# Four-layer convolution chain on one core: one output block a step, and a statistics pass that scales on GpSimd

## The chip, the cores and the metric

The kernel runs on one core of a Trainium2 chip. A core has TensorE (PE, matrix products into PSUM), VectorE (DVE), ScalarE (ACT), GpSimd (POOL), and SyncE (SP), whose queue issues nearly all DMAs here. The metric is device time in microseconds: 6498.27 us, the median of three runs (6492.53 to 6499.6). The profile is one further execution.

## The reference, cut to what matters

An image batch x of shape (4, 16, 512, 512) in float32 passes through four layers.

```python
x = layer0(x)    # depthwise 3x3 + windowed attention (8x8 windows) + MLP
# layer 1: fake-quantised 3x3 convolution, batch norm over the whole batch, clip
xq = fake_quant(x)                 # step = max|x| / 127, rounded
y  = conv3x3(xq, fake_quant(weight))
mean, var = mean(y, (0, 2, 3)), var(y, (0, 2, 3))
inv = gamma * rsqrt(var + 1e-5)
x  = clip(y * inv + (beta - mean * inv), 0, 6)
# layer 2: residual pair of convolutions
x  = conv3x3(relu(conv3x3(x, w1) + b1), w2) + b2 + x
# layer 3: convolution, then a two-layer pointwise network, residual
y  = conv3x3(x, conv_w)
x  = x + w2 @ relu(w1 @ y + b1) + b2       # 16 -> 128 -> 16 channels
```

Layer 1 needs the mean and variance of its convolution over the whole batch before any of its outputs can be normalised, so its convolution is computed twice: once for the statistics and once for the values.

## The kernel before, in words

The kernel has three stages. The first (`window_attention`, not touched) computes layer 0 and leaves its result in DRAM as `x1`, in 65 blocks of 128 partitions x 4 x 512 f32 (1 MB): `x1[mm]`. It also leaves per-partition maxima, from which `quant_step` gets the quantisation scale. A second path for large inputs isn't taken in the profiled run.

The **statistics pass** (the loop over `mm` in `conv_layers`, lines 992 to 1010) takes the 64 row blocks one after the other. `load(mm)` brings a block into one of four buffers (two tags, `x` and `o`, of two buffers each); `scaled(mm)` multiplies by the inverse step and adds a rounding constant, in place, on VectorE (L984, 128x2048); `rounded(mm)` takes the constant off again and writes bf16 into the ring `q` of three buffers, on ScalarE (L987). Then 24 turns (`_conv_turn`, L908) of four 32x32 products make the convolution of the block pair (mm, mm+1) in four PSUM banks; odd and even blocks use the two halves of PSUM. Four `bn_stats` (L1009) on VectorE read the banks. A load four blocks ahead is issued at the start of each turn of the loop. After the loop two edge blocks are loaded and scaled, and `bn_aggr` and some 1-column operations make `scale` and `shift`.

The **tail** (the loop over `t`, from `LATE, EARLY = ...` to the end of `conv_layers`) runs layers 1 to 3 as one software pipeline over the 64 blocks. A step has four groups, each of which is written by `group(conv, unit, between, at)`:

- group 1 ("x" below, after the tile that its convolution reads): layer 3's convolution, block t-4; its banks are copied to `y` by `done3`, two on VectorE, two on ScalarE;
- group 2 ("h"): layer 2's second convolution, block t-3; `done2` adds bias and `z` into `x` (four operations on VectorE, L1084). After it, `turned` issues 16 DMAs that transpose strips of `x` into `xi`, a ring of three;
- group 3 ("z"): layer 2's first convolution, block t-1; `done1` writes `h`, two on each engine;
- group 4 ("q"): layer 1's convolution again, block t, in bf16; `done0` writes `z` with Relu, scale and shift, all four strips on ScalarE (L1054). The upper clip follows in group 1 of the next step (`clipped`, L1060, VectorE).

All four convolutions use the same four banks, `conv_banks`. Each group also holds one *unit* of the pointwise network: the hidden layer of one strip of four, eight `hidden` calls of four products each (L1117) into `hid_banks`, used in turn, whose Relu goes to ScalarE five times (L1123) and to VectorE three times (L1125) out of eight. A group has 32 places on TensorE; `at` says which eight hold a hidden call, the other 24 being convolution turns. The place i also picks the row group i % 4 of the systolic array:

```python
    LATE, EARLY = range(4, 28, 3), (0, 1, 2, 3, 9, 12, 15, 18)
```

Groups 1 and 3 are LATE, groups 2 and 4 EARLY. When two units are ready, `outputs` (at the end of groups 2 and 4) makes their two output strips in `hid_banks[0:2]` (L1133, 16 products), and VectorE adds bias and the residual `xi` into a tile `o` (L1139); after the fourth strip SP stores the tile.

The order of the instructions on PE, DVE, ACT and SP is the order of the program text (a manual schedule); GpSimd, too, runs in order. Each engine stops at the first instruction whose semaphore isn't there yet.

Of the kernel before, what the change touches and what calls it, by code (L numbers as in the profile page):

```python
# [11 lines left out]
F32 = mybir.dt.float32  # L12
BF16 = mybir.dt.bfloat16
AF = mybir.ActivationFunctionType
ALU = mybir.AluOpType
# [8 lines left out]
B, C, H, W = 4, 16, 512, 512  # L24
P = 128
HR = H // 2
WP = W + 2
# [85 lines left out]
@with_exitstack  # L113
def conv_chain(ctx: ExitStack, tc: tile.TileContext, x, xw, mats, vecs, cqs, cws, hots, out):
    nc = tc.nc
    const = ctx.enter_context(tc.tile_pool(name="const", bufs=1))
    dram = ctx.enter_context(tc.tile_pool(name="dram", bufs=1, space=DRAM))

    x1 = dram.tile([M + 1, P, S, W], F32, name="x1")
    zero = const.tile([C, W], F32, name="zero")
    nc.vector.memset(zero, 0.0)
    for b in range(B):
        at = 32 * b
        nc.sync.dma_start(x1[0, at : at + C, 0], zero)
        nc.sync.dma_start(x1[M, at + C : at + 2 * C, S - 1], zero)
# [788 lines left out]
def conv_layers(ctx: ExitStack, tc, x1, out, cw, cq, sw, m, v, peak):  # L916
# [23 lines left out]
    banks = [ps.tile([P, W], F32, name=f"tb{i}") for i in range(8)]  # L940
    conv_banks, hid_banks = banks[0:4], banks[4:8]

    def ring(name, n, dt=F32):
        tiles = []
        for i in range(n):
            t = act.tile([P, 4, WP], dt, name=f"{name}{i}")
            nc.gpsimd.memset(t[:, :, 0 : WP : WP - 1], 0.0)
            tiles.append(t)
        return lambda mm: tiles[mm % n]

    qs = ring("q", 3, BF16)
    zs, hs, xs, xi, ys = ring("z", 3), ring("h", 2), ring("x", 2), ring("xi", 3), ring("y", 3)

    edge_b1 = act.tile([P, 2], F32, name="edge_b1")
# [14 lines left out]
    def inner(t):  # L969
        return t[:, :, 1 : W + 1]  # L970
# [4 lines left out]

    loaded = {}

    def load(mm, tag="x"):
        loaded[mm] = ld.tile([P, S, W], F32, tag=tag, name=f"tx{mm}")
        _load_pairs(nc, loaded[mm], x1, mm)  # L980

    def scaled(mm, at=slice(0, S)):
        t = loaded[mm][:, at]
        nc.vector.tensor_scalar(t, t, ix, ROUND, ALU.mult, ALU.add)  # L984

    def rounded(mm, at=slice(0, S)):
        nc.scalar.activation(  # L987
# [1 line left out]
        )  # L989


    tags = ("x", "o")
    for mm in range(4):
        load(mm, tags[mm % 2])
    sx, ix = quant_step(nc, act, act, peak, "x")
    for mm in range(2):
        scaled(mm)
        rounded(mm)
    for mm in range(M):
        if mm + 4 <= M:  # L1000
            load(mm + 4, tags[mm % 2])
        if mm + 2 <= M:
            scaled(mm + 2)
            rounded(mm + 2)
        p = banks[4 * (mm % 2) : 4 * (mm % 2) + 4]
        for turn in _turns():
            _conv_turn(nc, p, cq, (qs(mm), qs(mm + 1)), *turn)
        for b in range(B):
            nc.vector.bn_stats(stats[:, mm * B + b, :], p[b])  # L1009
    for mm in (-2, -1):  # L1010
        load(mm)
        scaled(mm)
        rounded(mm)
# [15 lines left out]

    own = act.tile([P, 2], F32, name="own")  # L1030
    nc.vector.bn_aggr(own, stats.rearrange("p r s -> p (r s)"))
    mean = over_strips(own[:, 0:1], "mean")
    off = act.tile([P, 1], F32, name="off")
    nc.vector.tensor_tensor(off, own[:, 0:1], mean, ALU.subtract)
# [15 lines left out]


    def done0(mm):
        for b, p in enumerate(conv_banks):
            nc.scalar.activation(  # L1054
                inner(zs(mm))[:, b], p, AF.Relu, bias=shift, scale=scale
            )

    def clipped(mm, b):
        z = inner(zs(mm))
        nc.vector.tensor_scalar(z[:, b], z[:, b], ACT_MAX, None, ALU.min)  # L1060
        if outside(mm) is not None:
            nc.vector.memset(z[_quad(outside(mm)), b], 0.0)

# [46 lines left out]
    waiting, outs = [], {}  # L1110

    def hidden(mm, s, par, b):

        k = next(count)
        p = hid_banks[k % 4]
        for c in range(4):
            nc.tensor.matmul(  # L1117
                p[_quad(c)], w1[_quad(b), 1 - par, 32 * c : 32 * c + 32],
                inner(ys(mm + par))[_quad(b), s, :], start=True, stop=True,
            )  # L1120
        hd = ld.tile([P, W], F32, tag="hid", name=f"hid{mm}_{s}_{par}_{b}", bufs=16)
        if k % 8 in (0, 2, 3, 5, 6):
            nc.scalar.activation(hd, p, AF.Relu, bias=v("l3_b1"))  # L1123
        else:
            nc.vector.tensor_scalar(hd, p, v("l3_b1"), 0.0, ALU.add, ALU.max)  # L1125
        return b, par, hd

    def outputs():

        for p in hid_banks[0:2]:  # L1130
            mm, s, hids = waiting.pop(0)
            for b, par, hd in hids:
                nc.tensor.matmul(  # L1133
                    p[_quad(b), :], w2[:, par], hd, start=par == 0, stop=par == 1
                )
            if s == 0:
                outs["o"] = ld.tile([P, S, W], F32, tag="o", name=f"o{mm}")
            o = outs["o"]
            nc.vector.scalar_tensor_tensor(  # L1139
                o[:, s, :], p, v("l3_b2"), inner(xi(mm))[:, s, :], ALU.add, ALU.add  # L1140
            )
            if s == S - 1:
                nc.sync.dma_start(out[mm], o)

    def group(conv, unit, between, at):


        turns, hids = iter(_turns() if conv else []), []
        for i in range(32):
            if i in at:  # L1150
                if unit:
                    hids.append(hidden(*unit, len(hids) // 4, i % 4))
                if between:
                    between.pop(0)()
            elif conv:
                _conv_turn(nc, conv_banks, conv[0], conv[1], *next(turns))
        for f in between:
            f()
        if conv:
# [14 lines left out]
    for t in range(-2, M + 7):  # L1174
        if t + 3 <= M + 2:
# [159 lines left out]
```

## Time and profile before

| what | before |
|---|---|
| median of the runs shown | 6498.27 us |
| time of the profiled execution | 6499.56 us |
| its span | 6497.8 us |
| PE / PE weight load | 6264.0 us (96%) / 3402.1 us (52%) |
| VectorE / ScalarE / GpSimd | 3186.5 us (49%) / 4179.7 us (64%) / 6.0 us |
| statistics pass, first scaling to last statistic | 3566.4 to 3805.4 us |
| first convolution of the tail to the end | 3817.9 to 6497.8 us |
| mean granted TensorE clock | 0.981 |

Busy times are sums over the whole span, and the three stages have different limits, so the shares of the whole say little of one stage. A row of the timeline gives the start in us from the span's start, the length, engine, line, operation, tiles (out<-in), shape and count, and in brackets how long the engine was idle before it and what ended that. Matmuls overlap in the array [...], and an f32 product of 512 columns leaves two records. A row of the waits gives the total in us, the number of times, and the longest.

### The profile page before, as it was taken

Reading aid. Unit: us, or ns where it says so; the run is one execution under the profiler, and the core shown is the slowest. Engines: PE = TensorE matmul, PEld = TensorE weight load, DVE = VectorE, ACT = ScalarE, POOL = GpSimd, SP = SyncE. Lnnn points to the kernel's source line nnn. Section 1 sums busy time; section 2 is a strip of 40 time slices with the busy share of each in tenths; the row PEclk is TensorE's granted clock in tenths of the full one; section 3 lists DMA queues with packets and bytes.
Section 4 is the critical chain, followed back from the end, with each engine's and each line's share of the span. In section 5 each row is a group of like instructions: output and inputs, shape, how many; then the busy total and the mean of one; then the engine's idle time right before and its main releaser. Section 6 shows DMA issues by size and latency. Waiting matters only on the chain. (4 is left out here: it accounts for less than half of the span.)

```text
span 6497.8 us, 317055 instructions
## 1 busy us (share of the span) xinstructions
PE 6264.0 (96%) x146976; PEld 3402.1 (52%) x146976; DVE 3186.5 (49%) x4640; ACT 4179.7 (64%) x5738; POOL 6.0 (0%) x26
## 2 busy tenths in 40 slices
PE   8999999999999999999997669999999999999999
PEld 5555555555555555555553335455555554555553
DVE  3444444444444444444443974544445554545554
ACT  5777777777777777777775544555555555555554
POOL 0000000000000000000000000000000000000000
PEclk9999999999999999999997879999999999999999
DMA  3333333333333333333322842222222222222221
GB/s 82 62 71 62 71 63 70 63 70 63 70 63 70 63 70 62 71 61 72 60 56 61 298 161 75 81 82 86 83 82 81 82 83 82 84 83 81 81 65 48
DMA packets 544390, 515.30 MB, mean 79 GB/s; under 512 B 349008, under 2 KB 480208, under 8 KB 514384
## 3 DMA queue, kind: packets, MB, share of 16 engines
q1 hardware_dynamic: 542768, 494.52, 29.2%
q8 instruction: 1154, 18.91, 1.2%
q14 instruction: 180, 1.47, 0.1%
q10 hardware_dynamic: 288, 0.39, 0.0%
HBM read 225.87 MB, written 134.48 MB: 55 GB/s over the span
## 5 line engine op out<-in xcount | busy, mean ns | idle before, releaser
L1123 ACT ACTIVATE hid<-tb,vec 128x512 f32<-128x512 f32 x1280 | 847.5, 687 | 1127.8 <-PE tb L1117 1126.5
L1117 PE MATMUL tb<-y,mat 32*32 32x512 f32 x16384 | 1567.9, 599 | 2.0 <-DVE o L1139 1.3
L367 ACT ACTIVATE e<-pair 128x1024 f32<-128x1024 f32 x1024 | 992.3, 1021 | 225.0 <-PE pair L359 224.3
L1125 DVE TENSOR_SCALAR hid<-tb,vec 128x512 f32<-128x512 f32 x768 | 575.3, 749 | 890.0 <-PE tb L1117 872.8
L295 PE MATMUL pair<-x,taps 32*32 32x512 f32 x18432 | 965.8, 605 | 1.9 <-ACT y L306 1.3
L416 PE MATMUL bank<-y,fc_e 32*32 32x512 f32 x8192 | 878.4, 607 | 3.7 <-ACT hid L421 3.2
L421 ACT ACTIVATE hid<-bank,f1b 128x512 f32<-128x512 f32 x1024 | 679.6, 686 | 298.8 <-PE bank L416 285.3
L351 DVE COPY yt<-bank 128x512 f32<-128x512 f32 x512 | 353.8, 691 | 906.1 <-PE bank L346 905.8
L359 PE MATMUL pair<-g,y 32*128 32x128 f32 x16384 | 651.2, 285 | 40.4 <-ACT e L367 39.3
L1117 PEld LDWEIGHTS tb<-y,mat 32*32 32x32 f32 x16384 | 496.4, 103 | 329.4 <-issue 185.0
L908 PE MATMUL tb<-z,cw 32*32 32x512 f32 x12864 | 640.4, 603 | 4.2 <-ACT z L1054 3.4
L359 PEld LDWEIGHTS pair<-g,y 32*128 32x128 f32 x16384 | 540.2, 186 | 186.8 <-ACT e L367 109.2
L908 PE MATMUL tb<-x,cw 32*32 32x512 f32 x12480 | 620.0, 597 | 1.5 <-ACT z L1054 1.5
L295 PEld LDWEIGHTS pair<-x,taps 32*32 32x32 f32 x18432 | 459.3, 103 | 286.3 <-issue 182.9
L908 PE MATMUL tb<-h,cw 32*32 32x512 f32 x12672 | 590.7, 601 | 1.8 <-ACT z L1054 1.5
L378 PE MATMUL bank<-e,yt 128*32 128x128 f32 x16384 | 555.3, 276 | 0.9 <-ACT r L393 0.9
L908 PE MATMUL tb<-q,cq 32*32 32x512 bf16 x12672 | 418.5, 424 | 138.4 <-ACT q L987 103.2
L383 PE MATMUL bank<-e,hot 128*32 128x512 f32 x4096 | 535.0, 593 | 0.0
L378 PEld LDWEIGHTS bank<-e,yt 128*32 128x32 f32 x16384 | 417.6, 109 | 108.1 <-DVE yt L351 52.8
L1133 PE MATMUL tb<-hid,mat 128*32 128x512 f32 x4096 | 471.1, 601 | 0.0
L429 DVE TENSOR_TENSOR xo<-bank,y 128x512 f32<-128x512 f32 x256 | 177.1, 692 | 547.2 <-PE bank L427 545.5
L346 PEld LDWEIGHTS bank<-mat,y 128*128 128x128 f32 x2048 | 215.3, 141 | 431.7 <-issue 378.1
(150 smaller groups left out, 6661.2 us busy)
## 6 DMA issues: line engine op xcount, KB each, us to landing
tx<-x SPq DMA_DIRECT2D x128, 1024.0 KB
x<-in_xw_dram SPq DMA_DIRECT2D x32, 2600.0 KB
y<-y SPq DMA_DIRECT2D x2048, 32.0 KB
xi<-x SPq DMA_DIRECT2D x1024, 64.0 KB
out_dram<-o SPq DMA_DIRECT2D x64, 1024.0 KB
x<-xo SPq DMA_DIRECT2D x2000, 32.0 KB
tx<-x SPq DMA_DIRECT2D x4, 768.0 KB
x<-xo SPq DMA_DIRECT2D x48, 24.0 KB
```

Source lines behind the costliest of these rows:

```text
L295: nc.tensor.matmul(bank(u)[quad(vv)], taps[quad(u), tap, :], xts[n // 2][quad(u), vv, dy : dy + WS, at : at + BW], start=tap == 0, stop=ta ...
L359: nc.tensor.matmul(bank(u)[:, P * jj : P * jj + P], y2[quad(u), vv, jl + jj].rearrange("p w t -> p (w t)"), g[quad(u), vv, jl + jj].rearra ...
L367: nc.scalar.activation(e[:, 2 * i : 2 * i + 2].rearrange("p u j t -> p u (j t)"), pairs[i], AF.Exp,)
L378: nc.tensor.matmul(b[quad(u), P * jj : P * jj + P], yt[:, jj, quad(u)], e[:, u, jj, :], start=True, stop=True,)
L383: nc.tensor.matmul(d[quad(u)], own, e[:, u].rearrange("p j t -> p (j t)"), start=True, stop=True,)
L416: nc.tensor.matmul(b[quad(k)], fc1[quad(vv), quad(k)], y[quad(vv), u, :], start=True, stop=True,)
L421: nc.scalar.activation(hd, b, AF.Gelu, bias=f1b)
L908: nc.tensor.matmul(p[i][_quad(j)], weights[_quad(i), side, dx, :], src[side][_quad(i), j, dx : dx + W], start=side == 0 and dx == 0, stop= ...
L1117: nc.tensor.matmul(p[_quad(c)], w1[_quad(b), 1 - par, 32 * c : 32 * c + 32], inner(ys(mm + par))[_quad(b), s, :], start=True, stop=True,)
L1123: nc.scalar.activation(hd, p, AF.Relu, bias=v("l3_b1"))
L1125: nc.vector.tensor_scalar(hd, p, v("l3_b1"), 0.0, ALU.add, ALU.max)
L1133: nc.tensor.matmul(p[_quad(b), :], w2[:, par], hd, start=par == 0, stop=par == 1)
```

## The change

In the tail, `outputs` is called once a step, when four units are ready, which is at the end of group 2. It uses all four hidden banks, adds into `xi` in place, and stores from there; the tile `o` is gone, and the ring of hidden tiles has 32 buffers instead of 16. Group 1 becomes EARLY. `done0` writes two strips on ScalarE and two on VectorE, without the lower clip, which `clipped` takes over in the same instruction.

In the statistics pass the scaling from block 2 on is done by GpSimd; the loads go to eight buffers, which are the tiles of the rings `y`, `xi` and `x` (idle in this pass), eight blocks ahead, and are issued at the end of each turn of the loop. The statistics live in the first tile of ring `h`. The zero borders of those rings are therefore written after the pass. A small tile of zeros is released early.

```diff
-    stats = act.tile([P, M * B, 6], F32, name="stats")
+    stats = rings["h"][0].rearrange("p s x -> p (s x)")[:, 0 : M * B * 6].rearrange(
+        "p (r s) -> p r s", s=6
+    )
...
-    def load(mm, tag="x"):
-        loaded[mm] = ld.tile([P, S, W], F32, tag=tag, name=f"tx{mm}")
+    def load(mm, t=None):
+        if t is None:
+            t = ld.tile([P, S, W], F32, tag="x", name=f"tx{mm}")
+        loaded[mm] = t
         _load_pairs(nc, loaded[mm], x1, mm)
 
-    def scaled(mm, at=slice(0, S)):
+    def scaled(mm, at=slice(0, S), engine=nc.vector):
         t = loaded[mm][:, at]
-        nc.vector.tensor_scalar(t, t, ix, ROUND, ALU.mult, ALU.add)
+        engine.tensor_scalar(t, t, ix, ROUND, ALU.mult, ALU.add)
...
-    tags = ("x", "o")
-    for mm in range(4):
-        load(mm, tags[mm % 2])
+    flat = [
+        t.rearrange("p s x -> p (s x)")[:, 0 : S * W].rearrange("p (s x) -> p s x", x=W)
+        for t in rings["y"] + rings["xi"] + rings["x"]
+    ]
+    AHEAD = len(flat)
+    for mm in range(AHEAD):
+        load(mm, flat[mm])
     sx, ix = quant_step(nc, act, act, peak, "x")
     for mm in range(2):
         scaled(mm)
         rounded(mm)
     for mm in range(M):
-        if mm + 4 <= M:
-            load(mm + 4, tags[mm % 2])
         if mm + 2 <= M:
-            scaled(mm + 2)
+            scaled(mm + 2, engine=nc.gpsimd)
             rounded(mm + 2)
         p = banks[4 * (mm % 2) : 4 * (mm % 2) + 4]
         for turn in _turns():
             _conv_turn(nc, p, cq, (qs(mm), qs(mm + 1)), *turn)
         for b in range(B):
             nc.vector.bn_stats(stats[:, mm * B + b, :], p[b])
+        if mm + AHEAD <= M:
+            load(mm + AHEAD, flat[mm % AHEAD])
+    for name in ("x", "xi", "y"):
+        border(name)
...
     def done0(mm):
+        z = inner(zs(mm))
         for b, p in enumerate(conv_banks):
-            nc.scalar.activation(
-                inner(zs(mm))[:, b], p, AF.Relu, bias=shift, scale=scale
-            )
+            if b % 2:
+                nc.vector.tensor_scalar(z[:, b], p, scale, shift, ALU.mult, ALU.add)
+            else:
+                nc.scalar.activation(z[:, b], p, AF.Identity, bias=shift, scale=scale)
 
     def clipped(mm, b):
         z = inner(zs(mm))
-        nc.vector.tensor_scalar(z[:, b], z[:, b], ACT_MAX, None, ALU.min)
+        nc.vector.tensor_scalar(z[:, b], z[:, b], ACT_MAX, 0.0, ALU.min, ALU.max)
...
-        hd = ld.tile([P, W], F32, tag="hid", name=f"hid{mm}_{s}_{par}_{b}", bufs=16)
+        hd = ld.tile([P, W], F32, tag="hid", name=f"hid{mm}_{s}_{par}_{b}", bufs=32)
...
     def outputs():
 
-        for p in hid_banks[0:2]:
+        for p in hid_banks:
             mm, s, hids = waiting.pop(0)
             for b, par, hd in hids:
                 nc.tensor.matmul(
                     p[_quad(b), :], w2[:, par], hd, start=par == 0, stop=par == 1
                 )
-            if s == 0:
-                outs["o"] = ld.tile([P, S, W], F32, tag="o", name=f"o{mm}")
-            o = outs["o"]
+            o = inner(xi(mm))
             nc.vector.scalar_tensor_tensor(
-                o[:, s, :], p, v("l3_b2"), inner(xi(mm))[:, s, :], ALU.add, ALU.add
+                o[:, s, :], p, v("l3_b2"), o[:, s, :], ALU.add, ALU.add
             )
-            if s == S - 1:
-                nc.sync.dma_start(out[mm], o)
+        nc.sync.dma_start(out[mm], o)
...
-        if len(waiting) == 2:
+        if len(waiting) == S:
             outputs()
...
         group(
             conv(2, xs, mm - 1, done3, mm) if 0 <= mm <= M else None,
             (t - 6, 2) if 0 <= t - 6 < M else None,
-            clip if -2 <= t - 1 <= M + 1 else [], LATE,
+            clip if -2 <= t - 1 <= M + 1 else [], EARLY,
         )
```

More of the change, by code (lines that the diff above doesn't have):

```diff
@@ L121, in conv_chain @@
     x1 = dram.tile([M + 1, P, S, W], F32, name="x1")
[L122 to L127, printed above, removed]
+    with tc.tile_pool(name="zeros", bufs=1) as one:
+        zero = one.tile([C, W], F32, name="zero")
+        nc.vector.memset(zero, 0.0)
+        for b in range(B):
+            at = 32 * b
+            nc.sync.dma_start(x1[0, at : at + C, 0], zero)
+            nc.sync.dma_start(x1[M, at + C : at + 2 * C, S - 1], zero)
     mat = const.tile([P, N_MAT], F32, name="mat")
@@ L941, in conv_layers, with border @@
     conv_banks, hid_banks = banks[0:4], banks[4:8]
+    rings = {}
     def ring(name, n, dt=F32):
-        tiles = []
-        for i in range(n):
-            t = act.tile([P, 4, WP], dt, name=f"{name}{i}")
+        tiles = rings[name] = [
+            act.tile([P, 4, WP], dt, name=f"{name}{i}") for i in range(n)
+        ]
+        return lambda mm: tiles[mm % n]
+    def border(name):
+        for t in rings[name]:
             nc.gpsimd.memset(t[:, :, 0 : WP : WP - 1], 0.0)
-            tiles.append(t)
-        return lambda mm: tiles[mm % n]
     qs = ring("q", 3, BF16)
     zs, hs, xs, xi, ys = ring("z", 3), ring("h", 2), ring("x", 2), ring("xi", 3), ring("y", 3)
+    for name in "qz":
+        border(name)
     edge_b1 = act.tile([P, 2], F32, name="edge_b1")
@@ L989, in rounded @@
         )
-    tags = ("x", "o")
-    for mm in range(4):
-        load(mm, tags[mm % 2])
+    flat = [
+        t.rearrange("p s x -> p (s x)")[:, 0 : S * W].rearrange("p (s x) -> p s x", x=W)
+        for t in rings["y"] + rings["xi"] + rings["x"]
+    ]
+    AHEAD = len(flat)
+    for mm in range(AHEAD):
+        load(mm, flat[mm])
     sx, ix = quant_step(nc, act, act, peak, "x")
@@ L1009, in conv_layers @@
             nc.vector.bn_stats(stats[:, mm * B + b, :], p[b])
+        if mm + AHEAD <= M:
+            load(mm + AHEAD, flat[mm % AHEAD])
+    for name in ("x", "xi", "y"):
+        border(name)
     for mm in (-2, -1):
@@ L1031, in conv_layers @@
     nc.vector.bn_aggr(own, stats.rearrange("p r s -> p (r s)"))
+    border("h")
     mean = over_strips(own[:, 0:1], "mean")
@@ L1109, in conv_layers @@
     count = iter(range(1 << 30))
-    waiting, outs = [], {}
+    waiting = []
     def hidden(mm, s, par, b):
```

## The prediction

> **What bounds the kernel now.** I read the page first (engine shares, the 40 slices, the chain), then the waits, DMA and timeline of the statistics pass, then TensorE's timeline over one step of the tail. From the page:
>
> ```profile
> span 6497.8 us, 317055 instructions
> PE   8999999999999999999997669999999999999999
> L279 POOL MEMSET y<- 128x4096 f32 x1 | 3.5, 3518 | 0.0
> ```
>
> TensorE is full everywhere except in slices 22 to 24, the statistics pass. So two readings are needed: what paces that pass, and what TensorE does in the tail, where it never rests. The waits, the DMA throughput (40 slices of 6.35 us) and the timeline of the pass (3561 to 3815 us):
>
> ```profile
> ACT q L987 <- DVE tx L984: 110.2, 47, 37.0
> PE tb L908 <- ACT q L987: 103.2, 50, 35.3
> GB/s 285 415 417 319 274 286 303 272 277 320 281 277 292 319 303 280 279 307 292 264 299 310 308 277 281 328 302 266 272 314 297 276 288 314 306 279 120 91 125 255
> 3594.79 1.27 DVE L984 TENSOR_SCALAR tx<-tx,inv_x 128x2048 f32<-128x2048 f32 x1
> 3595.98 2.48 DVE L1009 BATCH_NORM_STATS2 stats<-tb 128x6 f32<-128x512 f32 x4
> 3596.18 2.00 ACT L987 ACTIVATE q<-tx,unround 128x2048 bf16<-128x2048 f32 x1 [2.12 <-DVE tx L984]
> 3802.87 2.49 DVE L1009 BATCH_NORM_STATS2 stats<-tb 128x6 f32<-128x512 f32 x4 [1.32 <-PE tb L908]
> ```
>
> ScalarE waits for VectorE, TensorE for ScalarE: VectorE leads. It does one scaling (1.27 us) and four statistics (2.48 us, overlapping a little) a step, and the statistics of step 1 start at 3577.31, of step 63 at 3802.87: 3.64 us a step. The loads are not the limit: they run at about 290 GB/s, but at 415 to 417 in the two slices in which four were outstanding. From the first scaling (3566.38) to the last statistic (3805.36) the pass takes 239 us. The tail, one step on TensorE (starts of the groups; the first records of a group's own convolution or output block):
>
> ```profile
> 5083.41 0.69 PE L908 MATMUL tb<-x,cw 32*32 32x512 f32 x13
> 5093.09 0.66 PE L908 MATMUL tb<-h,cw 32*32 32x512 f32 x4
> 5102.01 0.64 PE L1133 MATMUL tb<-hid,mat 128*32 128x512 f32 x4
> 5105.59 0.76 PE L908 MATMUL tb<-z,cw 32*32 32x512 f32 x15
> 5115.26 0.41 PE L908 MATMUL tb<-q,cq 32*32 32x512 bf16 x4
> 5119.94 0.64 PE L1133 MATMUL tb<-hid,mat 128*32 128x512 f32 x4
> 5123.51 0.69 PE L908 MATMUL tb<-x,cw 32*32 32x512 f32 x13
> ```
>
> Step 40.10 us: group x 9.68, h 8.92, output block 3.58, z 9.67, q 4.68, output block 3.57. x, h and z have the same matrix work (24 convolution turns, 8 hidden products), yet the LATE groups x and z take 9.68 and the EARLY group h 8.92. ScalarE idles ahead of the hidden evictions in x (3.1 us before the first), so no product waits for one there, the 0.76 us is how the hidden products' row groups fall among the convolution's.
>
> **What the Trainium skill says.** "GPSIMD Engine Reference", § 3.1: a body of at most two arithmetic operations moves 1.03 cycles an element, while a two-input add of 2048 f32 measured 4497 ns; § 7 of the same page speaks of about 1.9 cycles for packed reads. The trace's only long GpSimd instruction, the memset of 4096 elements in 3518 ns, is 0.86 ns an element, which at the page's 1.2 GHz is 1.03 cycles; it reads nothing, so it agrees without deciding. "SBUF — State Buffer", § Who interferes with whom: GpSimd and VectorE share a port pair as an exclusive lock, but a VectorE operation with at most one SBUF input outside the two-port modes doesn't take it. The statistics read PSUM, so I expect no lock in the pass; no run here shows it yet.
>
> **The change part by part.**
>
> *Statistics pass.* 63 of the 65 scalings move to GpSimd (the first two and the two after the pass stay on VectorE). VectorE is left with 2.48 us a step, ScalarE 2.0, TensorE 96 products in about 1.7. The loads' floor is 1.049 MB at 417 GB/s = 2.51 us. GpSimd's scaling isn't in the trace. Lower bound, from memset: 128 elements took 205 ns and 4096 took 3518, so 2048 come to about 1.8 us. Upper bound: the page's two-input 4.5 us; between them 1.9 cycles, 3.2 us. I take 1.8, since one input is read and two operations done; then the loads set the step. New length: first landing 3566.4, 64 further tiles at 2.51 = 161, then the last tile's scaling 1.8, rounding 2.0, half a convolution 1.0, statistics 2.5: ends at 3734.7 instead of 3805.4, **71 us less**. At 3.2 us GpSimd sets the step: it starts at 3571.2 (third landing), 63 x 3.2 = 202, plus 5.5: 3779, 27 less. At 4.5: 3860, 55 more. The pass breaks even at 3.63 us.
> Eight buffers instead of four: a load waits for the rounding of the tile eight before it, about 4 us after that one landed, so some six loads stay queued; this only makes the 2.51 reachable. SP issues nothing else here. Left ring-border memsets (0.1 us each) follow the pass on GpSimd, hidden by the two scalings on VectorE and the 7.1 us aggregate. The two edge loads have their own buffers and are hidden behind the last tile's chain.
>
> *Group x from LATE to EARLY.* Saves 9.68 - 8.92 = 0.76 us in each of 64 steps if it packs as h does.
>
> *Output block moved.* The block after q goes; the one after h doubles to 7.14 us. Sum unchanged. But the block after q covered the evictions of z (L1054, four on ScalarE, 2.79 us from 5079.77). Now x's four leading hidden products cover 0.89 us. The eviction is split: ScalarE 2 x 0.69, VectorE 2 x 0.75 as in its other PSUM additions. VectorE is busy with the last hidden tile until 5080.09 (5079.34 + 0.75), so the fourth bank comes free at 5081.6, some 1.1 us after x's first turn would want it. Group h lives with nearly that today: its predecessor's copies (L1103 2 x 0.69 from 5092.88, L1105) free its fourth bank about 0.9 us late, inside the 8.92. So I charge 0.2 us a step for the slightly longer evictions and for the clips (0.42 each), which now queue in VectorE ahead of the second hidden tile as the scalings (0.48 each) do in h. Net 0.56 x 64 = **36 us less**. If the whole 1.1 us shows, the step gains nothing (-0.3 x 64 = 22 us worse); if nothing shows, 49 less.
> The first six steps have no outputs; there z's eviction is open today (3.0 us of TensorE idle at 3823.76), and halving it gives about 1 us in four of them: **4 less**.
>
> *Costed at nothing.* Relu's lower bound moves into the clip: same instruction. VectorE gains 2 x 0.75 us a step and is half busy. Hidden tiles live longer in 32 buffers; the next write comes after the block has read the first of them. Banks 0 to 3: z is LATE, its first hidden product comes four turns after the block. Output summed in place: the turned copies of the next tile into the same buffer, directly behind in SP's queue, must wait for the store. Store issued 8.1 us after h ends (block 7.14, eviction 0.75), 4.7 us to land (as the last one: issued 6493.1, end 6497.8), then sixteen copies in 14.3 us, then the next load: at 28 of a step of 39.5 us. The load has a step and a half before its scaling, the copies have three steps. If stores took 15 us longer, the load would begin to matter.
>
> **Sum**, against the profiled execution (6499.56 us, 1.3 above the median shown): 6499.6 - 71 - 36 - 4 = 6388.6; I say **6388**.
>
> **Rivals.**
> 1. *GpSimd paces the pass at 2.6 to 4.2 us.* For it: the 1.9 cycles; against: memset's rate. At 3.2: 6499.6 - 27 - 40 = 6433.
> 2. *Slower than before: GpSimd's scaling costs the two-input price or more.* With the tail's 40 us gained, the whole breaks even at (239 + 40 - 10.3) / 63 = 4.26 us; at 4.5 us it is 6499.6 + 55 - 40 = 6515, at 6 us about 6609. For it: software on the cores; against: one input only.
> 3. *The lost cover eats the tail's gain*: z's fourth bank and the second hidden tile late together. The step stays near 40.1: 6499.6 - 71 = 6429; for it: the queue on VectorE above; against: h does this today.
> 4. *Eight loads do not hold 417 GB/s* and stay at 290: the pass remains at 3.6 and only the tail gains: 6460. Against: the first four loads.
>
> **How the numbers follow.** Forecast 0.52; rival 1 0.22, rival 3 0.08, rival 4 0.03; rival 2 0.15 (a few hundredths of it within 0.2%, about 13 us, which is what a measurement of this kernel can tell from no change). Faster 0.83, same 0.03, slower 0.14. The range runs from 6366 (pass as forecast, tail 22 us better: no stall at x and a shorter h-like group) to 6460, which takes in rivals 1, 3 and 4; only rival 2 and small tails are left out.
>
> **What would show it.** Right: GpSimd rows of 128x2048 near 1.8 us, the pass's DMA row near 415 GB/s throughout, statistics 2.5 us apart, the pass some 71 us shorter; in the tail a step near 39.5 us with x about 9.1 and one block of 7.14. Wrong: ScalarE waiting for GpSimd in the pass, statistics further apart than 2.6 us; x as long as before, with TensorE or its weight loads waiting for VectorE's z; SP's load late, with VectorE's scaling waiting for it.

## The result and the profile after

| | before | after |
|---|---|---|
| median of five runs | 6497.87 us (6492.31 to 6499.6) | 6469.1 us (6465.19 to 6479.63) |
| profiled execution / span | 6499.56 / 6497.8 us | 6479.63 / 6477.8 us |
| first scaling to last statistic | 239.0 us | 258.8 us (forecast 168) |
| last statistic to the end | 2692.4 us | 2645.2 us (forecast 2652) |
| statistics, start to start, per step | 3.64 us | 3.93 us (forecast 2.51) |
| granted TensorE clock, 3600 to 3740 us | 0.82 | 0.71 |

The ratio after to before is 0.9963 [0.9952, 0.9974]: 29 us faster by the medians, not the 111 us of the forecast. The tail gave about what was expected. The statistics pass, which should have become 71 us shorter, became 20 us longer. (In the two profiled executions the attention stage, which the change doesn't touch, runs 8.7 us apart after its first 200 us; over all the profiled executions of this study the first scaling starts between 3566.4 and 3578.4 us. So the stages are compared here, not the spans. The three parts do add up: +7.5 until the first scaling, +19.8, -47.2 make the -19.9 us between the two executions.)

From the page of the kernel after: the span, the engines' busy time and instructions, TensorE's row and its granted clock in 40 slices, and the instruction queue's row (packets, MB, share of 16 engines).

```profile
span 6477.8 us, 317011 instructions
PE 6215.1 (96%) x146976; PEld 3422.4 (53%) x146976; DVE 3208.4 (50%) x4713; ACT 4062.8 (63%) x5602; POOL 130.9 (2%) x89
PE   8999999999999999999998569999999999999999
PEclk9999999999999999999998679999999999999999
q8 instruction: 1154, 18.91, 1.2%
```

TensorE's dip in slices 22 to 24 is still there: 8, 5 and 6 tenths where before had 7, 6 and 6. The last row is one that the prediction didn't read; it is the one that explains the pass.

The group of GpSimd's scaling in the kernel after (busy time in all, mean ns of one, idle time before them and what ended it):

```profile
L996 POOL TENSOR_SCALAR xi<-xi,inv_x 128x2048 f32<-128x2048 f32 x24 | 47.4, 1974 | 43.8 <-DMA xi<-x 43.8
```

One scaling takes 1.97 us, near the 1.8 us of the forecast, and GpSimd then waits for its data. It paces nothing. What does is in the waits of the pass, 3600 to 3790 us (total us, times, longest), kernel after:

```profile
PEld L909 <- issue: 103.2, 59, 4.5
ACT q L999 <- PE tb L909: 94.2, 38, 4.2
PE tb L909 <- issue: 79.8, 35, 4.2
DVE h L1024 <- PE tb L909: 76.5, 36, 3.9
POOL xi L996 <- DMA xi<-x: 41.2, 20, 3.8
```

and of the kernel before, same window:

```profile
PEld L908 <- issue: 109.7, 90, 2.5
ACT q L987 <- DVE tx L984: 60.8, 38, 2.1
PE tb L908 <- ACT q L987: 58.4, 42, 2.1
PE tb L908 <- issue: 16.7, 17, 1.5
```

The weight loads (PEld) wait for "issue" about as long in both; the products don't. Before, the order of waiting was TensorE on ScalarE on VectorE. After, it is reversed: ScalarE and VectorE wait for TensorE, GpSimd waits for the loads, whose buffers ScalarE frees; and TensorE, at the head of it all, waits 79.8 us in 190 for "issue", that is for nothing with a semaphore. TensorE's timeline of the kernel after shows the form of these waits (start, length, engine, line, operation, tiles, count, and in brackets the idle time before):

```profile
3683.39 3.64 PE L909 MATMUL tb<-q,cq 32*32 32x512 bf16 x128 [2.23 <-issue]
3688.51 3.64 PE L909 MATMUL tb<-q,cq 32*32 32x512 bf16 x128 [1.47 <-issue]
3699.29 3.58 PE L909 MATMUL tb<-q,cq 32*32 32x512 bf16 x128 [2.56 <-issue]
3703.58 2.06 PE L909 MATMUL tb<-q,cq 32*32 32x512 bf16 x128 [0.71 <-issue]
```

A step has 96 products, but TensorE stops after 128. The transfers of the instruction queue show why. Each is 16384 bytes, and its 18.91 MB over the whole execution, divided by the 146976 products and as many weight loads of the page, are 64.3 bytes for each of them: one transfer holds about 128 products and their 128 weight loads. The starts of six of them, set against the starts of the bursts:

```
fetch starts    burst starts    between
3681.02         3683.39         2.37
3686.27         3688.51         2.24
3691.46         3693.90         2.44
3696.88         3699.29         2.41
3701.32         3703.58         2.26
3707.24         3709.52         2.28
```

So TensorE's program is itself DMA traffic, one fetch for every 128 products, and 0.75 of a fetch a step. In the pass after, a fetch comes every 5.43 us: 0.75 x 5.43 = 4.07 us. That is the step in this stretch: 3296 products in 3600 to 3740 us (shown further below) make 140 x 96 / 3296 = 4.08 us; the 3.93 is the mean over the whole pass. This agreement is only counting, since every kernel fetches what it executes. That TensorE waits for the fetches is seen in the waits themselves: in 3600 to 3790 us there are 35 fetches and 35 waits of TensorE for "issue"; every wait ends 2.2 to 2.6 us after a fetch has started, exactly 128 products after the wait before it. The share of the loads is in the DMA view of the same window:

```profile
DMA packets 7296, 53.38 MB, mean 281 GB/s; under 512 B 815, under 2 KB 815, under 8 KB 815
q1 hardware_dynamic: 7257, 52.78, 74.0%
q8 instruction: 35, 0.57, 1.1%
```

The fetches are 1.1% of the engines' time and too few to notice beside 74.0% of loads, and 281 GB/s is less than the 417 that the forecast took.

The tail of the kernel after, one step on TensorE, by the first records of each group (the two columns ahead are start and length):

```profile
5009.99 0.61 PE L909 MATMUL tb<-x,cw 32*32 32x512 f32 x1
5018.73 0.66 PE L909 MATMUL tb<-h,cw 32*32 32x512 f32 x4
5027.17 0.64 PE L1155 MATMUL tb<-hid,mat 128*32 128x512 f32 x4
5034.18 0.73 PE L909 MATMUL tb<-z,cw 32*32 32x512 f32 x15
5043.86 0.41 PE L909 MATMUL tb<-q,cq 32*32 32x512 bf16 x4
5049.30 0.61 PE L909 MATMUL tb<-x,cw 32*32 32x512 f32 x1
```

39.31 us instead of 40.10 (forecast 39.54): x 8.74, h 8.44, one output block of 7.01, z 9.68, q 5.44.

### The profile page after: what moved, and what is told of

The parts are those of the page before. It is cut to its first block, busy times and chain, and to the rows that moved or that the text cites. A ratio compares the mean times of both kernels' runs of the same rounds, so it can differ in the third digit from the quotient of the medians.

```text
span 6477.8 us, 317011 instructions
## 1 busy us (share of the span) xinstructions
PE 6215.1 (96%) x146976; PEld 3422.4 (53%) x146976; DVE 3208.4 (50%) x4713; ACT 4062.8 (63%) x5602; POOL 130.9 (2%) x89
## 3 DMA queue, kind: packets, MB, share of 16 engines
q8 instruction: 1154, 18.91, 1.2%
## 5 line engine op out<-in xcount | busy, mean ns | idle before, releaser
L1139 PE MATMUL tb<-y,mat 32*32 32x512 f32 x16384 | 1494.9, 596 | 6.5 <-issue 6.0
L1145 ACT ACTIVATE hid<-tb,vec 128x512 f32<-128x512 f32 x1280 | 829.5, 688 | 1068.3 <-PE tb L1139 1066.1
L1139 PEld LDWEIGHTS tb<-y,mat 32*32 32x32 f32 x16384 | 464.1, 103 | 270.7 <-issue 152.5
L909 PE MATMUL tb<-h,cw 32*32 32x512 f32 x12672 | 571.1, 597 | 3.5 <-ACT z L1078 1.5
L909 PE MATMUL tb<-x,cw 32*32 32x512 f32 x12480 | 562.5, 597 | 2.0 <-ACT z L1078 1.4
L1155 PE MATMUL tb<-hid,mat 128*32 128x512 f32 x4096 | 452.7, 594 | 0.0
```

The source lines that it names most:

```text
L909: nc.tensor.matmul(p[i][_quad(j)], weights[_quad(i), side, dx, :], src[side][_quad(i), j, dx : dx + W], start=side == 0 and dx == 0, stop= ...
L1139: nc.tensor.matmul(p[_quad(c)], w1[_quad(b), 1 - par, 32 * c : 32 * c + 32], inner(ys(mm + par))[_quad(b), s, :], start=True, stop=True,)
L1155: nc.tensor.matmul(p[_quad(b), :], w2[:, par], hd, start=par == 0, stop=par == 1)
```

## The experiments

The statistics pass was taken apart first. Three theories were on the table:

- **Theory 1**: TensorE waits for its instructions, because the fetches are late beside the loads.
- **Theory 2**: the lower granted clock makes TensorE slow.
- **Theory 3**: the loads set the step after all, at the rate that they hold here.

In every table "step" is the mean distance of the statistics, "fetch" the mean distance of two instruction fetches in the middle of the pass, "tail" the time from the last statistic to the end. These three are of one profiled execution; where a time has no ratio beside it, the kernel was executed once.

### Each half of the change alone

The old pass with the new tail (on top of the kernel after):

```diff
-    ]
+    ][0:4]
...
-            scaled(mm + 2, engine=nc.gpsimd)
+            scaled(mm + 2)
```

> The changed kernel with four load buffers and the scaling on VectorE, so the pass works as before and only the tail is new. If the gain is the tail's and the pass is what took it back: pass about 239 us, tail about 2645 us, time 6498 - 47 = 6451. If the pass is at 259 us here too, its loss is not from GpSimd or the eight loads but from something else that the change moves (where the buffers lie): 6470.

And the new pass with the old tail: the kernel before, with `rings`, `border`, `flat`, the loads, the statistics in `h` and the GpSimd scaling of the kernel after.

```diff
+    flat = [
+        t.rearrange("p s x -> p (s x)")[:, 0 : S * W].rearrange("p (s x) -> p s x", x=W)
+        for t in rings["y"] + rings["xi"] + rings["x"]
+    ]
...
-            scaled(mm + 2)
+            scaled(mm + 2, engine=nc.gpsimd)
...
+        if mm + AHEAD <= M:
+            load(mm + AHEAD, flat[mm % AHEAD])
```

> The kernel before with the new statistics pass alone. Additive reading: pass about 259 us, 6498 + 20 = 6518. If the pass was only slow in the one profiled execution: 6498 - 71 = 6427.

| | time | ratio to before (6494.13 us) | step | tail |
|---|---|---|---|---|
| old pass, new tail | 6449.18 us | 0.9929 [0.9913, 0.9946] | 3.64 us | 2630.5 us |
| new pass, old tail | 6512.66 us | 1.0025 [1.0013, 1.0036] | 3.79 us | 2689.0 us |

The tail alone is worth 45 us, the pass alone costs 19; together -26, where the whole change measured -29. As far as these times can tell, the two halves don't disturb each other. The half without the new pass is, with the variant of eight buffers on VectorE further below (6450.49 us), the fastest complete kernel of this study. The new pass takes 3.79 us a step here and 3.93 in the kernel after, with the same code: a difference of 0.14 us between two single executions says little.

### Without the loads

The loads after the first eight are left out, so that the pass works on the same eight tiles again and again; GpSimd takes a minimum instead of a product so that the values stay bounded.

```diff
-        engine.tensor_scalar(t, t, ix, ROUND, ALU.mult, ALU.add)
+        engine.tensor_scalar(
+            t, t, ix, ROUND, ALU.min if engine is nc.gpsimd else ALU.mult, ALU.add
+        )
...
-            load(mm + AHEAD, flat[mm % AHEAD])
+            loaded[mm + AHEAD] = flat[mm % AHEAD]
```

> The changed kernel, but only the first eight blocks are loaded in the statistics pass; the later ones take the old buffers again (the scaling on GpSimd is min and add, so that values stay finite). It leaves the loads out. Theory 1, TensorE starves for instructions because their 16 KB fetches queue behind the loads: TensorE's unexplained waits nearly go, a step falls from 3.95 us to about 2.7 us or less, pass about 175 us. Theory 2, TensorE's lower granted clock (0.70 instead of 0.83) makes the convolutions slow: the pass stays near 255 us. Theory 3, the loads themselves are late: pass about 165 us, limited by VectorE's 2.4 us, and TensorE waits for ScalarE rather than for nothing.

The run took 6677.08 us with a step of 7.02 us, and says nothing on the fetches, because the substitute was no like for like. Its timeline on GpSimd, three operations in a row:

```profile
3684.95 21.46 POOL L996 TENSOR_SCALAR y<-y,inv_x 128x2048 f32<-128x2048 f32 x3
```

7.15 us each where product and addition take 1.97. GpSimd paced this pass, and TensorE's wait for "issue" was 0.6 us in 3600 to 3790. That it vanishes when TensorE has time is in line with theory 1, but is no test of it. So again, with the same two operations and a factor of one half:

```diff
+    half = act.tile([P, 1], F32, name="half")
+    nc.vector.memset(half, 0.5)
...
+        by = half if engine is nc.gpsimd else ix
-        engine.tensor_scalar(t, t, ix, ROUND, ALU.mult, ALU.add)
+        engine.tensor_scalar(t, t, by, ROUND, ALU.mult, ALU.add)
...
-            load(mm + AHEAD, flat[mm % AHEAD])
+            loaded[mm + AHEAD] = flat[mm % AHEAD]
```

> Again only the first eight blocks are loaded in the statistics pass, but GpSimd keeps multiply and add (by 0.5 in place of the inverse step, so that values stay finite), which took 1.97 us; the loads are left out and the scale is another. Theory 1 (instruction fetches queue behind the loads): a fetch comes back sooner than the 5.4 us between fetches in the changed kernel, TensorE's unexplained waits shrink from about 80 us in 190 to under 20, a step is 2.4 to 2.8 us, the pass 155 to 180 us. Theory 2 (the lower granted clock): a step stays near 3.9 us.

6404.64 us, a step of 2.83 us and a fetch every 3.76 us (0.75 x 3.76 = 2.82). Windows of this kernel: window, length, busy PE, PEld, DVE, ACT, POOL (instructions), granted clock, DMA share, GB/s:

```profile
3600.00:3740.00 140.00, 93.17 (x4784) 62.51 (x4770) 122.09 (x200) 98.77 (x51) 103.72 (x54) 0.93 0.02 5
```

The same of the kernel after, and below it of the kernel before:

```profile
3600.00:3740.00 140.00, 80.72 (x3296) 52.94 (x3275) 84.27 (x136) 69.15 (x35) 76.17 (x39) 0.71 0.75 283
3600.00:3740.00 140.00, 84.81 (x3664) 51.18 (x3679) 139.03 (x195) 77.95 (x39) 0.00 (x0) 0.82 0.83 294
```

Without the loads, 4784 products instead of 3296 go through in the same time. And still the waits of 3600 to 3790 us have

```profile
PE tb L909 <- issue: 51.6, 42, 2.0
```

so even with the DMA engines idle TensorE starves at times: a fetch every 3.76 us seems to be near a limit of its own. The clock (theory 2) explains at most the smaller part of the difference. For 96 products TensorE is busy 80.72 x 96 / 3296 = 2.35 us with the loads and 93.17 x 96 / 4784 = 1.87 us without, 0.48 us apart. It is idle 4.08 - 2.35 = 1.73 against 2.81 - 1.87 = 0.94 us: 0.79 of the 1.27 us by which the steps of the two windows differ.

### Half of the bytes

As the last, but with two of a tile's four strips loaded each time, 512 KB instead of 1024.

```diff
             loaded[mm + AHEAD] = flat[mm % AHEAD]
+            if mm + AHEAD < M:
+                nc.sync.dma_start(loaded[mm + AHEAD][:, 0:2], x1[mm + AHEAD][:, 0:2])
```

> The changed kernel with GpSimd scaling by 0.5, and from the ninth block on only two of the four strips loaded (512 KB a step); it leaves half of those loads out. If the traffic delays the fetches in proportion: a step between 2.83 us (no loads) and 3.93 us (all), about 3.3 us. If it is enough that a load is outstanding: 3.9 us.

6431.88 us; step 3.33, fetch 4.51 us. The window:

```profile
3600.00:3740.00 140.00, 85.99 (x4052) 58.07 (x4048) 103.04 (x168) 83.92 (x43) 88.43 (x45) 0.84 0.50 161
```

Half of the bytes lies in the middle between none and all: steps 2.83, 3.33, 3.93. Its clock, 0.84, is nearly that of the pass before (0.82), but the comparison decides nothing on theory 2, because there VectorE set the step of 3.64.

### Fewer products

Of the three columns of the kernel window in the pass, the middle one is left out: 64 products a step instead of 96, with all loads.

```diff
-        for turn in _turns():
-            _conv_turn(nc, p, cq, (qs(mm), qs(mm + 1)), *turn)
+        for side, dx, i in [(s, d, i) for s in range(2) for d in range(0, 3, 2) for i in range(4)]:
+            _conv_turn(nc, p, cq, (qs(mm), qs(mm + 1)), side, dx, i)
```

> The changed kernel with the middle column taps left out of the statistics convolution: 64 products a step instead of 96, loads as they are. It leaves a third of that convolution out. Theory 1: a step needs 64/128 of a fetch instead of 96/128, so at about 5.3 us a fetch a step falls from 3.95 to about 2.7 us, pass about 180 us. Theory 2: the products are 1.4 us a step of busy time instead of 2.1, at most 0.7 us less: about 3.3 us, pass 215. Theory 3 (loads set the step): unchanged, pass 259.

6401.12 us, step 2.90 us; the window:

```profile
3600.00:3740.00 140.00, 94.22 (x3072) 43.03 (x3040) 117.04 (x192) 95.68 (x48) 100.68 (x51) 0.67 0.98 384
```

The loads ran at 384 GB/s, 0.98 of the DMA engines. So the 281 GB/s of the kernel after isn't what these loads can hold, and theory 3 falls. (Here they are near their own limit: 1.049 MB at 384 GB/s is 2.73 us of the 2.90.) The clock, 0.67, is lower than that of the kernel after, and the step is 1.03 us shorter, where theory 2 allowed 0.7: it falls as the main cause. A step needs 0.5 of a fetch now, and a fetch came every 5.87 us: 0.5 x 5.87 = 2.94, by the same counting as above. What the run shows is that the interval of the fetches, 5.43 us in the kernel after, got no shorter when a third of a step's products was taken away; so the step fell to 0.74 of its length with two thirds of the program.

Put in order of traffic, the TensorE that is waiting for instructions gets them ever later:

| | DMA, 3600 to 3740 us | fetch every | of it, fetch start to products (median) |
|---|---|---|---|
| no reloads | 5 GB/s | 3.76 us | 2.4 us |
| half of the bytes | 161 GB/s | 4.51 us | 2.4 us |
| kernel after | 283 GB/s | 5.43 us | 2.4 us |
| two thirds of the products | 384 GB/s | 5.87 us | 2.4 us |

The last column doesn't move. So a fetch that has begun is as fast as ever; the time is lost before its packet begins. The clock falls down this table, too (0.93, 0.84, 0.71, 0.67), so a rival has to be looked at: slower products might ask for the next fetch later. The traces speak against it. The clock record of these windows switches between 1.0 and 0.5. In the kernel after, the nine fetch intervals with a mean clock under 0.67 are 5.21 us long and the six with one over 0.83 are 5.39; without loads it is 3.65 (five) and 3.75 us (31). At one and the same traffic, a low clock doesn't delay the fetches. That a fetch stands in a queue behind load packets is then the natural reading. It is argued, not shown: the trace has the starts of packets, not the time at which they were asked for. Nor is the mean traffic all of it: the passes below run at 273 to 295 GB/s, and their fetches come every 4.85 to 5.44 us in no order of traffic.

### Depth, packet size, and who scales

If it is the traffic, neither the number of buffers nor the size of the packets should matter much; if it is the depth of the queue, four or three loads ahead should be as good as the kernel before. Four edits of the kernel after, each alone. Loads four ahead:

```diff
-    ]
+    ][0:4]
```

> The changed kernel with four load buffers instead of eight, scaling on GpSimd. If the number of loads outstanding delays the fetches: fetches closer than 5.4 us apart, a step of 3.2 to 3.6 us, pass about 215 us. If any steady stream of loads does it: a step of 3.9 us as with eight.

Loads three ahead, `[0:3]` in the same place:

> The changed kernel with three load buffers. If fewer loads outstanding let fetches through: under 3.7 us a step. If not: 3.9 us as with four and eight, or more, since a load is then asked for later.

VectorE scales, with all eight buffers:

```diff
-            scaled(mm + 2, engine=nc.gpsimd)
+            scaled(mm + 2)
```

> The changed kernel with the scaling back on VectorE, eight load buffers kept. VectorE then paces at 3.64 us a step, a fetch every 4.8 us is enough, and after the first blocks one load at a time is outstanding: pass about 232 us from the first statistic, as before. If eight buffers alone starve TensorE, also in this pace: a step of 3.9 us, pass 250.

Rows of 2 KB in the buffers instead of flattened ones of 8 KB:

```diff
-        t.rearrange("p s x -> p (s x)")[:, 0 : S * W].rearrange("p (s x) -> p s x", x=W)
+        inner(t)
```

> The changed kernel, the eight buffers taken as four rows of 2 KB in each partition (the rings' inner columns) instead of one row of 8 KB: the same bytes in packets of 2 KB (0.09 us each on an engine) instead of 8 KB (0.31 us). If a fetch waits behind a fixed number of packets ahead of it, it waits a quarter as long: a step of 2.6 to 3.2 us, pass 170 to 205 us. If it waits for a share of the bytes: no change, a step of 3.9 us.

| | time | step | fetch |
|---|---|---|---|
| kernel after, eight ahead | 6469.1 us | 3.93 us | 5.43 us |
| four ahead | 6466.77 us | 3.93 us | 5.22 us |
| three ahead | 6463.72 us | 3.75 us | 5.05 us |
| rows of 2 KB | 6478.43 us | 3.98 us | 5.44 us |
| VectorE scales, eight buffers | 6450.49 us | 3.72 us | 4.85 us |

Depth isn't the cause: eight and four are alike. Three ahead is 0.18 us a step shorter, little more than the 0.14 us between two executions of the same pass above. Packets of 2 KB change nothing. What brings the pass back near 3.64 us is only that VectorE scales. Eight buffers with VectorE take 0.08 us a step more than the old pass, so the extra buffers gained nothing.

The window of four ahead:

```profile
3600.00:3740.00 140.00, 81.00 (x3440) 53.75 (x3426) 87.92 (x143) 70.43 (x37) 70.69 (x37) 0.76 0.73 273
```

Its clock is 0.76 against the 0.71 of the kernel after; in this stretch it does 3440 products instead of 3296, over the whole pass its step is the same.

### A mixture

If a TensorE that is paced a little suffers less, giving GpSimd only some of the scalings should find an optimum.

```diff
-            scaled(mm + 2, engine=nc.gpsimd)
+            scaled(mm + 2, engine=nc.gpsimd if mm % 2 else nc.vector)
```

and, for a third of them, `if mm % 3 == 2`.

> The changed kernel with every second scaling on GpSimd and the others on VectorE, eight buffers. VectorE then needs about 2.4 + 0.64 = 3.05 us a step and a fetch every 4.05 us. If a steady stream of loads still lets a fetch through in about 4 us, and the 5.4 us came from starving TensorE and loads that bunch: a step of 3.1 to 3.3 us, pass from the first statistic 195 to 210 us, time 6420. If TensorE cannot be fed faster than a chunk in about 5 us beside the loads: 3.8 us, pass about 243 us, time 6460, no better than the scaling on VectorE.

> The same with every third scaling on GpSimd: VectorE 2.4 + 0.85 = 3.25 us a step, a fetch every 4.35 us. Steady loads are enough: 3.3 us, pass 210 us. A floor of about 5 us a fetch: 3.75 us, pass 240.

| | time | ratio to before (6493.05 us) | step | fetch |
|---|---|---|---|---|
| every other | 6470.14 us | 0.9959 [0.9945, 0.9973] | 3.88 us | 5.10 us |
| every third | 6482.02 us | no interval | 4.00 us | 5.27 us |

A miss: there is no optimum between. With a third of the scalings on GpSimd VectorE has 0.67 x 1.27 + 2.48 = 3.3 us of work a step, and the pass takes 4.00, no less than with all of them on GpSimd. Nor do the two engines hold each other up much: beside GpSimd's, VectorE's scalings took 1.39 us in the mean instead of 1.27 (one 2.61), and GpSimd's stayed within 0.01 us. That VectorE's pace alone keeps the fetches on time isn't the whole of it, then. What distinguishes the old pass, in which a fetch comes every 4.81 us at 294 GB/s while starving passes get one only every 5.1 to 5.4, stays open. (Bunching of the loads was considered; no run tested it.)

### The tail

Two steps of the prediction for the tail are tested on the kernel with the old pass and new tail: group x back to LATE,

```diff
-            clip if -2 <= t - 1 <= M + 1 else [], EARLY,
+            clip if -2 <= t - 1 <= M + 1 else [], LATE,
```

and all four evictions of z back on ScalarE.

```diff
-            if b % 2:
+            if b > 3:
                 nc.vector.tensor_scalar(z[:, b], p, scale, shift, ALU.mult, ALU.add)
```

> Old pass, new tail, but group x keeps its LATE places. The prediction's step: EARLY against LATE is worth 0.76 us less 0.2 for the uncovered eviction: a step of about 39.3 + 0.6 = 39.9 us, time about 6449 + 36 = 6485. Rival: the gain is in the single output block (one start and end of a block less), and LATE, whose first four places are convolution turns, only shows the eviction that has lost its cover: more than 41 us a step.

> Old pass, new tail, but all four z evictions on ScalarE, as in the kernel before, without the output block behind them. The last bank then comes free 2.8 us after group q instead of 1.8: if the lost cover counts fully, a step of about 40.3 us and 6510 us; if the order of the row groups absorbs it as in group h, under 0.3 us a step, 6460.

| | time | step of the tail | tail | q start to x start | x start to h start |
|---|---|---|---|---|---|
| new tail | 6449.18 us | 39.29 us | 2630.5 us | 5.44 us | 8.73 us |
| group x LATE | 6554.87 us | 40.72 us | 2735.8 us | 5.44 us | 9.68 us |
| z on ScalarE | 6567.02 us | 40.55 us | 2745.6 us | 5.44 us | 10.00 us |

Both reversals cost more than the step that the prediction worked out for them: 105 and 115 us. With x LATE, x is back at the 9.68 us of the kernel before, and h at 8.92 instead of 8.44, together 1.43 us a step; x alone is 0.95. With z on ScalarE, the first turns of x wait. The kernel with z on ScalarE, TensorE at the start of x:

```profile
5003.67 3.07 PE L909 MATMUL tb<-x,cw 32*32 32x512 f32 x37
5006.22 0.63 PE L1139 MATMUL tb<-y,mat 32*32 32x512 f32 x4
```

and the kernel after at the same place:

```profile
5010.02 1.70 PE L909 MATMUL tb<-x,cw 32*32 32x512 f32 x29
5011.24 0.73 PE L1139 MATMUL tb<-y,mat 32*32 32x512 f32 x4
```

The next hidden products start 2.55 us into the convolution turns instead of 1.22. What is waited for stands in the waits of 4600 to 6000 us, some 34 steps; first the kernel with z on ScalarE, then the kernel after:

```profile
PEld tb L909 <- ACT z L1078: 62.9, 136, 0.5
PEld tb L909 <- ACT z L1078: 19.6, 70, 0.3
```

The difference of 43.3 us is 1.3 us a step. This is the cover that the output block after q used to give, and the split on two engines is what makes its removal harmless. In both runs the means of the steps are about 41.2 us, 0.5 and 0.7 over their regular steps; the rest of the 105 and 115 us is in these longer steps, which weren't followed up.

## Why the prediction was right and wrong

**What bounds the kernel before** was read rightly: VectorE leads the pass, TensorE the tail.

**The statistics pass: wrong.** It was to give 71 of the 111 us and cost 20. The step that failed is "then the loads set the step", with "TensorE 96 products in about 1.7" in the sum ahead of it. The duration fits a burst at full clock (128 products in 2.06 us at 3703.58), though at the mean clock of 0.71 TensorE was busy for 2.35 us a step; what was missing is that TensorE's instructions are traffic and can come late. 96 products and 96 weight loads are 12 KB of program a step, fetched 16 KB at a time through the same DMA engines. Beside the loads a fetch took 5.43 us from one to the next, so the pass settled at 3.93 us a step instead of 2.51, and 258.8 us instead of 168. "The loads are not the limit" of the old pass was right, but what came next after VectorE wasn't the loads: without any reload the pass still took 2.83 us a step, of which VectorE's statistics explain 2.48. The evidence for the late fetches stood in the trace of before: TensorE waited for "issue" 17 times and 16.7 us in 3600 to 3790 us, beside 58.4 us for ScalarE, and each of these 17 waits ends 2.2 to 2.5 us after an instruction fetch has started. The prediction showed the larger line and passed over the smaller. Why the fetches come late beside the loads stays open in its last link, as said above.

**GpSimd's scaling** was right: 1.97 us against 1.8. It was the term with the widest bounds, 1.8 to 4.5 us, and most of the prediction's doubt went there. The memset's rate was the better guide, and the price that "GPSIMD Engine Reference", § 3.1 gives for two arithmetic operations, 1.03 cycles an element, nearly agrees: 1974 ns for 2048 elements is 1.16 cycles at the page's 1.2 GHz, with the start of the instruction in it. The two-input price doesn't apply. It is no price for any pair of operations, though: minimum and addition on the same operands took 7.15 us, 4.2 cycles an element. That the statistics wouldn't be held up by GpSimd was right as well: one of them takes 0.68 us in the mean before and after.

**Eight buffers** "only make the 2.51 reachable": they don't. Four (3.93) and three (3.75) are no worse.

**Group x from LATE to EARLY, with the output block moved**: predicted -0.56 us a step, measured -0.80 on the regular steps. Where it came from is a different split: q and x together 14.36 to 14.18 (their boundary moved, since x's leading hidden products now start inside q's time), h 8.92 to 8.44, output blocks 7.15 to 7.01. The undone edit, x LATE, shows that x and h gain together (0.95 and 0.48 us): h was taken as the unchanged pattern, and it gained too. The 0.2 us charged for the evictions of z, now without the block's cover, was about right for the split: x is 0.3 us longer than h. Put back on one engine, they cost 1.27 us a step.

**Sum of the tail**: -40 predicted, -47.2 between the two profiled executions, -45 by the medians of the half alone. In the twelve profiled executions that have all of the new tail it took 2630.5 to 2646.8 us, in the two with the old one 2692.4 and 2689.0, so the gain is 42 to 62 us. The forecast is near in size, but not in its parts, and in so far it is luck. From the last statistic to the start of x in the first full step, the kernel after is 13.5 us shorter, where "4 less" was given; the drain after the last x is 7.9 us shorter, where nothing was; the full steps between make -25.8 instead of -36. As to these: of 58 steps in the middle, 17 are clearly longer than 39.31, up to 41.3, and the mean is 39.72; before, all 58 lie between 40.09 and 40.18. In 4600 to 6000 us TensorE has six gaps of more than 0.15 us; all six lie in longer steps and end 2.2 to 2.5 us after the start of a fetch. That is the signature of the pass, but the six make 4.0 us of an excess of 12.3, and no run tested it there.

**Costed at nothing**, and rightly so: SP. The timeline of SP's queue in the kernel after (SPq: the issues of its DMAs):

```profile
5035.11 0.60 SPq L1162 DMA_DIRECT2D out_dram<-xi  x1
5039.76 12.02 SPq L1117 DMA_DIRECT2D xi<-x  x16
5051.87 1.64 SPq L892 DMA_DIRECT2D tx<-x  x1
```

The store is issued 7.9 us after h ends, the turned copies behind it start 4.7 us later, and the next load 24.7 us after h's end, where 28 was forecast.

**The rivals.** GpSimd at 2.6 to 4.2 us (rival 1) and at 4.26 and more (rival 2) didn't occur. The lost cover (rival 3) didn't either, owing to the split. Rival 4 named what is seen, loads that stay at about 290 GB/s and a pass of some 3.6 us a step, with 0.03 of chance and 6460 us; the measured time is 6469. But its cause is wrong as well: the loads held 384 GB/s beside two thirds of the products; they run at 281 because their buffers don't come free sooner. A rival with a reason, "TensorE's own instructions are late", was missing, and with it any case in which the pass becomes longer than before while GpSimd is fast.

## What to carry to other kernels

A stage of many small matrix products has a need that no list of its loads and stores shows: its program. Divide the products and weight loads of a step into fetches (here 128 and 128 in 16 KB), and before relieving the engine that paces such a stage look at TensorE's waits for "issue": if they are there while another engine paces it, they may be the next bound, as they were here, and here more traffic of loads made them worse. When an output block that covers an eviction is moved away, shorten the eviction in the same edit: splitting it over two engines was worth 1.3 us a step here.

## What the hardware showed unexpectedly

- TensorE's instructions come in transfers of 16 KB, 128 products with 128 weight loads; the products that wait for one follow its start by 2.4 us, loaded or not. With the DMA engines otherwise idle, TensorE got one every 3.76 us in this pass, at 161, 283 and 384 GB/s of loads every 4.51, 5.43 and 5.87 us.
- On GpSimd, minimum and addition on 128x2048 f32 took 7.2 us, product and addition 1.97 us, with the same operands.
- In these windows the granted clock mostly rose with the product rate (2016 products in 140 us, with the minimum on GpSimd: 0.60; 3072: 0.67; 3296: 0.71; 4052: 0.84; 4784: 0.93), though not strictly: with every second scaling on GpSimd 3448 products went with 0.68, four ahead 3440 with 0.76. A low clock doesn't mean a long step: 0.67 went with 2.90 us.
